# Filler matmuls behind V products split into four of 32 columns, logits by cluster moved there, and x2's block turns sent from another queue

## The chip, the cores and the metric

The kernel runs on one core of one Trainium2 chip. The metric is device time in microseconds (us), as the median of the runs. The profile is of one execution of the same program.

## The reference

Input x has 8 x 512 tokens of 1024 features, all float32. Four steps are each added to the running x, and each works on a layer norm of it:

```python
x = x + attn_a(layernorm(x))   # softmax attention, 32 heads of 32, qkv and output projection
x = x + ffn(layernorm(x))      # dense 1024x1024, masked
x = x + attn_b(layernorm(x))   # causal sigmoid attention, 4 heads of 256, q = k = v = the normed x, bound by sign vectors
x = x + ffn(layernorm(x))      # the same dense layer
```

The mask of the ffn comes from 64 clusters: softmax(10 x centroids^T) per token, hits are the entries above 0.01; a token with no hit gets zeros, and an output feature whose cluster no token hits is zero as well. So the logits by cluster of every token are needed before the first row of ffn's output can be gated.

## The kernel before, in words

Tokens are cut into 32 tiles of 128 (partitions), four tiles to a batch. Five stages follow each other: softmax attention (to about 2600 us of the profile), its tail, the first dense layer (to about 3113 us), sigmoid attention (to about 3465 us), the second dense layer.

**Softmax attention** runs over 64 units: a unit is one batch and one group of four heads (`GH` = 4, `HD_A` = 32). The order on TensorE is written out by hand in the loop over `n`. For each of the four key tiles i of unit n it has: `rows_step` (scores of unit n + 1 with queries as rows, L830, whose maximum VectorE takes, L831), filler, `keys_step` (scores of unit n with keys as rows, L858 and L861, whose exp ScalarE takes, L863), and filler again. At i = 0 `values_step` (V products `av`, L885) and `normalize` (the sums of the softmax `den`, L897, and VectorE's division, L900 on) of unit n - 1 stand between `keys_step` and the filler; at i = 2 `values_step` of unit n. Scores use the array as four row groups of 32 rows (32*128 in the profile); V products and `den` use it as four column groups of 32 columns (128*32), one for each head, each head writing its own 32 partitions of one PSUM tile.

**The filler** is a queue of pieces, each with a weight in us; `between` takes as many as the place's share (`FILLER_SHARES`) allows. In it lie the projections of unit n + 2 (`project_pieces`; q and k L638, V L659, in the first batch L574 and L593), the output projection of the batch before (`out_pair`, L768), and for each finished tile of the attention its norm, its turn (`turn_pieces`, L277) and its cluster logits (`Clusters.pieces`): `by_cluster` puts `logitsT` in two column groups of 64 (128*64, L307), ScalarE copies it (`lT`), and `by_token` (L313) adds the halves and turns them. These products are 128*128. Their PSUM tiles come from the ring `ps_m` of three, which `den` shares.

**The dense layers** run over 16 pairs of tiles: seven products of Strassen-Winograd form (k = 0 to 6), each of four chunks of 512 columns (L1181). ScalarE copies the first into `u` (L148), VectorE adds the others (L142). PSUM has five buffers here. While pair p is multiplied, the tiles of pair p - 1 are normed on ScalarE (`scale`, L240), transposed in 32x32 blocks on VectorE (`turn_blocks`, L1411) and sent to DRAM as `xT2`, four DMAs for each tile, from ScalarE's queue (L1415). SyncE (SP) carries the loads: `load_turned` (L1112) and `load_x` (L1118) of pair p + 2, and at the last pair `load_head` (L1220) and `load_x2` (L1438) for the sigmoid attention. VectorE forms the sums of a pair's left side (L1128) and gates the finished pair (L1194 to L1196).

**Sigmoid attention** runs over 32 heads: scores `csc` (L1240), sigmoid on ScalarE into `at` (L1245), GpSimd's causal select (L1248), values `o` (L1259). `keys` scales the next head's `k` on ScalarE (L1232); `value` makes `cn` on ScalarE and GpSimd (L1226). The last two block turns of x2 are made in steps s = 2 and 3.

Of the kernel before, what the change touches and what calls it, by code (L numbers as in the profile page):

```python
# [22 lines left out]
P = 128  # L23
# [261 lines left out]
        return [(0.45, half(0)), (0.45, half(1))]  # L285


class Clusters:


# [3 lines left out]
        self.hits = fixed.tile([P, NCL], F32, name=f"hits_{name}")  # L294
        self.logits = {}

    def pieces(self, t, xT, later=None):

        nc, (b, i), st, ps_m = self.stage.nc, divmod(t, TPB), {}, self.stage.ps_m

        def by_cluster():
            acc = ps_m.tile([P, P], F32, tag="mm", name="logitsT")
            for c in range(NC):
                half = ts(c % 2, NCL)
                nc.tensor.matmul(acc[half, :], self.cT[:, c, :], xT()[:, c, :], start=(c < 2), stop=(c >= NC - 2))  # L307
            st["lT"] = self.pool.tile([P, P], F32, tag="lT", name=f"lT_{self.name}_{t}")
            nc.scalar.copy(st["lT"], acc)

        def by_token():
            acc = ps_m.tile([P, NCL], F32, tag="mm", name="logits")
            nc.tensor.matmul(acc, st["lT"], self.stage.cst.twice, start=True, stop=True)  # L313
            if i == 0:
                self.logits[b] = self.pool.tile([P, TPB, NCL], F32, tag="lg", name=f"lg_{self.name}_{b}")
            nc.scalar.activation(self.logits[b][:, i, :], acc, AF.Copy, scale=INV_TEMP)
            if i == TPB - 1:
                steps = self.softmax(b)
                if later is None:
                    for step in steps:  # L320
                        step()
                else:
                    later(steps)

        return [(1.3, by_cluster), (0.25, by_token)]
# [61 lines left out]
def softmax_attention(tc, cst, stage, filler, clusters, pools, dr, late, args):  # L387
# [54 lines left out]

    once = [partial(ow_source, RIGHT[k], c) for k in UPPER for c in range(half)]
    ows = Stream(nc, owpool, OW_BUFS, [P, S], "ow", once * (2 * B - 1))
    used, side, tiles, held = {"w": 0}, deque(), deque(), []

    def first_norm():

# [27 lines left out]
    def norm_tasks(b):  # L476
# [48 lines left out]
            scaled[4:],  # L525
        ]

    first_w = {}

    def load_first(g, kinds):  # L530
# [34 lines left out]
    def first_pieces(n):  # L565


        g, st, pieces = n, state.setdefault(n, {}), []

        def qk(t, c):  # L570
            def go():
                if c == 0:
                    st["acc"] = ps_m.tile([P, S], F32, tag="mm", name="mm")
                nc.tensor.matmul(  # L574
                    st["acc"], first_w[t, g, c // half][:, c % half, :], xTs[0][:, c, :],
                    start=(c == 0), stop=(c == NC - 1),
                )
                if c == NC - 1:
                    o = st["qk"[t]] = qkpool.tile([P, S], F32, tag=f"qk{t}", name=f"qk{t}_{n}")
                    bias = qkvb_s[:, t * NC + g : t * NC + g + 1]  # L580
                    if t == 0:
                        nc.vector.tensor_scalar(o, st["acc"], bias, None, ALU.add)
                    else:
                        nc.scalar.activation(o, st["acc"], AF.Identity, bias=bias)

            return go

        def v(i, k):
            def go():
                if i == 0 and k == 0:  # L590
                    st["acc"] = ps_m.tile([P, TPB, P], F32, tag="mm", name="mm")
                for c in range(half):
                    nc.tensor.matmul(  # L593
                        st["acc"][:, i, :], xTs[0][:, k * half + c, ts(i, P)], first_w[2, g, k][:, c, :],
                        start=(k == 0 and c == 0), stop=(k == 1 and c == half - 1),
                    )
                if i == TPB - 1 and k == 1:
                    st["v"] = vpool.tile([P, TPB, P], F32, tag="v", name=f"v_{n}")
                    nc.scalar.copy(st["v"], st["acc"])

            return go

        def sums():
            qk = [first_w.pop((t, g, k)) for k in range(2) for t in range(2)]
            steps = sum_weights("qk", g, *qk) + [partial(load_first, g + 2, (0, 1))]
            if g % 2:
                steps += sum_weights("v", g // 2, *(first_w.pop((2, g - 1 + m, k)) for k in range(2) for m in range(2)))
            steps.append(partial(load_first, g + 2, (2,)))
            side.extendleft(reversed(steps))

        for t in range(2):
            pieces += [(0.86, qk(t, c)) for c in range(NC)]
        return pieces + [(0.87, v(i, k)) for i in range(TPB) for k in range(2)] + [(0.0, sums)]
# [9 lines left out]
    def project_pieces(n):  # L623
# [9 lines left out]
        def qk(k, c0):  # L633
            def go():
                if c0 == 0:
                    st["acc"] = ps_m.tile([P, 2 * P], F32, tag="mm", name="mm")
                for c in (c0, c0 + 1):
                    nc.tensor.matmul(  # L638
                        st["acc"], weights.tiles[base + EARLY.index(k)][:, c, :], left(k)[:, c, :],
                        start=(c == 0), stop=(c == half - 1),  # L640
                    )
                if c0:
                    if k == 0:
                        for t in range(2):
                            st["qk"[t]] = qkpool.tile([P, S], F32, tag=f"qk{t}", name=f"qk{t}_{n}")
                    q, kk = st["q"], st["k"]
                    bias = [qkvb_s[:, t * NC + g : t * NC + g + 1] for t in range(2)]
                    gather(nc, k, st["acc"], q[:, lo], kk[:, lo], q[:, hi], kk[:, hi], bias, early=True)
                    weights.done(base + EARLY.index(k))

            return go

        def v(k, at, i):
            def go():
# [1 line left out]
                    st["acc"] = ps_m.tile([P, 2, P], F32, tag="mm", name="mm")  # L656
                w = weights.tiles[at]
                for c in range(half):
                    nc.tensor.matmul(  # L659
                        st["acc"][:, i, :], left(k)[:, c, ts(i, P)], w[:, c, :], start=(c == 0), stop=(c == half - 1)  # L660
                    )
                if i == 1:
# [38 lines left out]
    def out_pair(q, pools, base, last):  # L701
# [61 lines left out]
        def mm(idx, c):  # L763
            def go():
                k, at = UPPER[idx], base + idx * half + c
                if c == 0:
                    st["acc"] = ps_m.tile([P, S], F32, tag="mm", name="mm")
                nc.tensor.matmul(  # L768
                    st["acc"], st["left"][LEFT[k]][:, c, :], ows.tiles[at], start=(c == 0), stop=(c == half - 1)
                )  # L770
                if last:
                    ows.done(at)
                if c == half - 1:
                    done(k)

            return go
# [23 lines left out]
    def tile_pieces(t, r):  # L800
# [13 lines left out]
        def keep():  # L814
# [1 line left out]

        return (
            stage.norm_pieces(lambda: r, xn, scalar=True) + stage.turn_pieces(xn, xT, keep, vector=False),
            clusters.pieces(t, xT, None if t >= NTILE - TPB else held.extend),
        )  # L820

    def rows_step(n, qt):
# [84 lines left out]

    places = [0]

    def between(sides=True):  # L910

        if sides:
            for _ in range(-(-len(side) // places[0])):
                side.popleft()()
            places[0] -= 1
        filler.take()

    def mix_tile(near=False):
        norm, logits = tiles.popleft()
        filler.mix(norm[:2], 0 if near else 2, 2 if near else 5)  # L920
        filler.mix(norm[2:], 9 if near else 14, 3)
        filler.mix(logits, 16 if near else 22, 4)

    def weave(pieces, products):

# [28 lines left out]
    for n in range(units):  # L954
# [13 lines left out]
            filler.add(weave(project_pieces(ahead), products), mark=ahead)  # L968
        else:
            filler.add(weave([], products))  # L970
        if tiles:
            mix_tile(n == units - 1)
        for c in OUT_SUMS.get(n, ()):
            side.extend(ow_sum_tasks(c))
        if b + 1 < B:
# [10 lines left out]
        for i in range(TPB):  # L986
# [12 lines left out]
                sum_step(n, i)  # L999
            if i == 0 and n > 0:  # L1000
                values_step(n - 1, 1)
                normalize(n - 1)
            if i == 2:
                values_step(n, 0)
            between(False)
        if n + 1 < units:
            split_max(n + 1)
        if ahead < units:
# [264 lines left out]
def block_body(tc, long, dr, args, out):  # L1273
# [117 lines left out]
    def x2_pair(p):  # L1391
# [10 lines left out]
        for t in tiles:  # L1402
            xn, xT, _ = turned_tile(t, dr.xT2)
            scale = (0.0, lambda xn=xn, t=t: stage.rescale(xn(), dense1.x[t], keep(t)))
            turns.append((scale, (0.0, partial(turn_blocks, t, xn, xT))))
        return turns

    def turn_blocks(t, xn, xT):

        blocks = xT().rearrange("p c t -> p (c t)")  # L1410
        nc.vector.transpose(blocks, xn())  # L1411
        dst = dr.xT2[t].rearrange("(j q) (c i t) -> i q c j t", j=P // 32, c=NC, i=P // 32)
        for i in range(P // 32):
            src = blocks[ts(i, 32)].rearrange("q (c j t) -> q c j t", c=NC, j=P // 32)
            nc.scalar.dma_start(dst[i], src)  # L1415

    def x3_pieces(t):

# [28 lines left out]
    for p in range(pairs):  # L1447
        pieces = dense1.products(p) if p > 1 else left_over if p == 1 else []
        for k, (scale, turn) in enumerate(turns):
            pieces.insert(max(len(pieces) - 8, 14) + 5 * k, turn)  # L1450
        at = max(len(pieces) - 19, 12)
        pieces[at:at] = [scale for scale, _ in turns]
        if p == 1:
# [30 lines left out]
    for s in range(heads + 1):  # L1484
# [23 lines left out]
            by_token = turned[1][1:]  # L1508
        run_held()
        if s in (2, 3):  # L1510
            run([turns[s - 2][1]])
        t = s + TPB - 1
        if TPB <= t < NTILE:
            sig.value(t, x2, keep(t))
# [88 lines left out]
```

## Time and profile before

| | us |
|---|---|
| median of 3 runs | 3873.09 (3871.13 to 3873.58) |
| profiled execution | 3871.99 |
| its span | 3870.2 |
| TensorE busy (matmuls) | 3810.0 |
| VectorE busy | 2507.8 |
| ScalarE busy | 942.1 |
| GpSimd busy | 620.1 |
| granted TensorE clock | 0.996 |

A span is from the first to the last instruction; 1.8 us of the profiled execution lie around it. PE is TensorE's matmuls, PEld its weight loads, DVE VectorE, ACT ScalarE, POOL GpSimd, SP SyncE. An x16 behind a row of matmuls counts what the hardware ran: a float32 product is two passes, each with a weight load. Ends of matmuls are modelled, so that rows overlap; starts are exact.

### The profile page before, as it was taken

What the parts mean: (1) busy time and instruction counts of PE and PEld (TensorE: products, weight loads), DVE (VectorE), ACT (ScalarE), POOL (GpSimd) and SP (SyncE); (2) the same over time, 40 slices, a digit from 0 to 9 for tenths busy, and PEclk for the clock granted to TensorE, in tenths of its full rate; (3) what the DMA queues carried; (4) which work ended last, traced back from release to release, by engine and by line L of the source; (5) the groups of instructions that cost most, each with busy time, mean ns of one, the idle gap of its engine ahead of it and who ended that gap; (6) DMA issues with size and microseconds to landing.
All of it is one profiled execution on the core that took longest, in us unless ns stands there. A gap on an engine that the chain in (4) does not pass through costs nothing.

```text
span 3870.2 us, 51693 instructions
## 1 busy us (share of the span) xinstructions
PE 3810.0 (98%) x20526; PEld 2151.8 (56%) x20526; DVE 2507.8 (65%) x3471; ACT 942.1 (24%) x1044; POOL 620.1 (16%) x609
## 2 busy tenths in 40 slices
PE   8999999999999999999999999998999999999999
PEld 4445555655655555655655556543444467774444
DVE  4667676666666666766766666665788744455666
ACT  1222222222222232222322223222111144430000
POOL 1222111111111111111111111111000045530000
PEclk9999999999999999999999999999999999999999
DMA  5435444544544444454354443347566655554332
GB/s 166 125 110 169 125 140 139 169 135 132 177 132 133 146 147 155 127 173 147 121 166 145 131 136 117 110 148 239 154 172 175 183 157 191 191 188 138 130 131 98
DMA packets 574624, 577.57 MB, mean 149 GB/s; under 512 B 168232, under 2 KB 420144, under 8 KB 574384
## 3 DMA queue, kind: packets, MB, share of 16 engines
q1 hardware_dynamic: 408704, 440.81, 36.7%
q0 software_dynamic: 28240, 100.94, 6.6%
q10 hardware_dynamic: 137440, 32.52, 3.8%
q8 instruction: 164, 2.69, 0.3%
q14 instruction: 76, 0.62, 0.0%
HBM read 439.90 MB, written 134.25 MB: 148 GB/s over the span
## 4 chain that ended last, share of the span: by engine, by line
PE 95%; DVE 2%; DMA 2%; ACT 1%; issue 0%; SPq 0%; ACTq 0%; POOL 0%; DVEq 0%; POOLq 0%
PE dense L1181 19%; PE mm L638 19%; PE mm L768 10%; PE mm L659 9%; PE sc L858 7%; PE sc L830 7%; PE av L885 6%; PE csc L1240 4%; PE o L1259 4%; PE mm L574 3%; PE logitsT L307 2%; PE tp L277 2%; PE sc L861 1%; PE den L897 1%; PE mm L593 1%
## 5 line engine op out<-in xcount | busy, mean ns | idle before, releaser
L831 DVE TENSOR_REDUCE nmax<-sc 128x4 f32<-128x2048 f32 x256 | 586.0, 2289 | 306.0 <-PE sc L830 305.0
L863 ACT ACTIVATE pT<-sc 128x2048 f32<-128x2048 f32 x256 | 480.8, 1878 | 1051.6 <-PE sc L861 1051.6
L638 PE MATMUL mm<-xT,w 128*128 128x256 f32 x1792 | 440.0, 389 | 1.4 <-DVE rden L900 1.4
L872 POOL TENSOR_TENSOR sum<-pT,pT 128x1024 f32<-128x1024 f32 x128 | 304.7, 2407 | 763.3 <-ACT pT L863 763.3
L638 PEld LDWEIGHTS mm<-xT,w 128*128 128x128 f32 x1792 | 327.1, 191 | 128.3 <-DVE rest L838 35.6
L638 PE MATMUL mm<-s,w 128*128 128x256 f32 x1344 | 332.1, 390 | 0.0
L638 PEld LDWEIGHTS mm<-s,w 128*128 128x128 f32 x1344 | 244.1, 190 | 134.3 <-issue 95.7
L858 PE MATMUL sc<-qk,qk 32*128 32x512 f32 x2048 | 292.7, 641 | 8.9 <-DVE nmax L831 8.4
L874 DVE TENSOR_TENSOR sum<-sum,pT 128x2048 f32<-128x2048 f32 x128 | 292.0, 2281 | 0.8 <-ACT pT L863 0.8
L830 PE MATMUL sc<-qk,qk 32*128 32x512 f32 x2048 | 291.9, 640 | 0.1
L142 DVE TENSOR_TENSOR u<-dense,u 128x512 f32<-128x512 f32 x223 | 149.6, 688 | 189.6 <-PE dense L1181 166.4
L768 PE MATMUL mm<-ow,ctxT 128*128 128x512 f32 x512 | 252.1, 612 | 0.5 <-DMA ow<-o_T 0.5
L885 PE MATMUL av<-pT,v 128*32 128x512 f32 x2048 | 246.2, 598 | 0.0
L1181 PE MATMUL dense<-sum,s 128*128 128x512 f32 x512 | 233.8, 597 | 6.5 <-ACT u L148 3.9
L659 PEld LDWEIGHTS mm<-w,xT 128*128 128x128 f32 x1792 | 209.1, 192 | 52.9 <-issue 33.8
L144 DVE SCALAR_TENSOR_TENSOR qk<-mm,qkvb_s,qk 128x256 f32<-128x256 f32 x224 | 107.5, 480 | 188.5 <-PE mm L638 186.2
L659 PE MATMUL mm<-w,xT 128*128 128x128 f32 x1792 | 220.5, 278 | 0.0
L768 PE MATMUL mm<-ow,c 128*128 128x512 f32 x360 | 172.6, 610 | 2.8 <-DMA ow<-o_T 2.8
L1181 PE MATMUL dense<-wT_s,dT_b 128*128 128x512 f32 x384 | 171.4, 593 | 1.6 <-DMA dT_b<-xT 1.6
L1181 PE MATMUL dense<-wT_s,dT_a 128*128 128x512 f32 x384 | 171.0, 593 | 0.0
L1181 PEld LDWEIGHTS dense<-sum,s 128*128 128x128 f32 x512 | 97.0, 191 | 128.5 <-issue 112.7
L659 PEld LDWEIGHTS mm<-w,s 128*128 128x128 f32 x1344 | 155.8, 192 | 20.1 <-issue 19.4
(229 smaller groups left out, 4688.9 us busy)
## 6 DMA issues: line engine op xcount, KB each, us to landing
w<-in_qkvw SPq DMA_DIRECT2D x252, 256.0 KB, 2.9
ow<-o_T SPq DMA_DIRECT2D x240, 256.0 KB, 3.5
w<-qk_T SPq DMA_DIRECT2D x224, 256.0 KB, 2.6
ow<-in_ow SPq DMA_DIRECT2D x180, 256.0 KB, 3.0
w<-v_T SPq DMA_DIRECT2D x112, 256.0 KB, 2.7
x<-in_x SPq DMA_DIRECT2D x32, 512.0 KB, 5.0
xT<-nT POOLq DMA_DIRECT2D x32, 512.0 KB, 4.2
dT_a<-xT SPq DMA_DIRECT2D x32, 512.0 KB, 5.5
```

The lines of the kernel that those rows point to most:

```text
L638: nc.tensor.matmul(st["acc"], weights.tiles[base + EARLY.index(k)][:, c, :], left(k)[:, c, :], start=(c == 0), stop=(c == half - 1),)
L659: nc.tensor.matmul(st["acc"][:, i, :], left(k)[:, c, ts(i, P)], w[:, c, :], start=(c == 0), stop=(c == half - 1))
L768: nc.tensor.matmul(st["acc"], st["left"][LEFT[k]][:, c, :], ows.tiles[at], start=(c == 0), stop=(c == half - 1))
L830: nc.tensor.matmul(sc[:, h, :], st["q"][rows, ts(qt, P)], st["k"][rows, :], start=True, stop=True)
L831: nc.vector.tensor_reduce(st["nmax"][:, qt, :], sc, AX.X, ALU.max, negate=True)
L858: nc.tensor.matmul(sc[:, h, :], st["k"][rows, ts(kt, P)], st["q"][rows, :], start=True, stop=False)
L863: nc.scalar.activation(pT, sc, AF.Exp, scale=SCALE_A)
L872: nc.gpsimd.tensor_tensor(st["sum"][:, h, :], st["pT", 0][:, h, :], st["pT", 1][:, h, :], ALU.add)
L874: nc.vector.tensor_tensor(st["sum"], st["sum"], st["pT", kt], ALU.add)
L885: nc.tensor.matmul(st["av"][rows, :], st["v"][:, kt, rows], pT[:, h, :], start=(kt == 0), stop=(kt == TPB - 1))
L1181: nc.tensor.matmul(st["acc"], st["left"][LEFT[k]][:, c, :], self.w[RIGHT[k]][:, c, :], start=(c == 0), stop=(c == half - 1),)
L1240: nc.tensor.matmul(sc[:, AT_OFF[i] : AT_OFF[i] + n], k[:, c, ts(i, P)], xT[:, c, i * P :], start=(c == 0), stop=(c == 1),)
```

## The change

Three things are edited.

1. `product` stands in for the matmul of the projections (q, k, V and output). Where `narrow` is set, it issues four matmuls, one for each group of 32 columns of the left side, into the four 32-partition parts of the same PSUM tile. `between` sets it for the third filler place of i = 0 (behind `values_step` and `normalize`) and that of i = 2 (behind `values_step`), from unit 1 on.
2. In the attention's units `by_cluster` is no longer mixed into the filler of its unit. It waits (`waiting`, `ready`) for i = 0 of the next unit and runs there between `values_step` and `normalize`; `by_token` is put six pieces on in the filler. For the attention's tiles `logitsT` is made in four column groups of 32 (`width=HD_A`).
3. The block turns of x2 become two pieces, `turn` (VectorE's transpose) and `send` (the four DMAs, now from SyncE). In a pair's 28 products the turns stand two to three products earlier, the sends three pieces behind them.

```diff
+    def block_pieces(self, x, box, dram):
+        n = P // 32
+        def turn():
+            self.nc.vector.transpose(box().rearrange("p c t -> p (c t)"), x())
+        def send():
+            blocks = box().rearrange("p c t -> p (c t)")
+            dst = dram.rearrange("(j q) (c i t) -> i q c j t", j=n, c=NC, i=n)
+            for i in range(n):
+                self.nc.sync.dma_start(dst[i], blocks[ts(i, 32)].rearrange("q (c j t) -> q c j t", c=NC, j=n))
+        return [(0.0, turn), (0.0, send)]
...
-    def pieces(self, t, xT, later=None):
+    def pieces(self, t, xT, later=None, width=NCL):
...
             for c in range(NC):
-                half = ts(c % 2, NCL)
-                nc.tensor.matmul(acc[half, :], self.cT[:, c, :], xT()[:, c, :], start=(c < 2), stop=(c >= NC - 2))
+                for j in range(NCL // width):
+                    rows = ts(c % 2 * (NCL // width) + j, width)
+                    nc.tensor.matmul(
+                        acc[rows, :], self.cT[:, c, ts(j, width)], xT()[:, c, :], start=(c < 2), stop=(c >= NC - 2)
+                    )
...
+    narrow = [False]
+
+    def product(out, lhsT, rhs, **flags):
+        if narrow[0]:
+            for j in range(GH):
+                nc.tensor.matmul(out[ts(j, HD_A)], lhsT[:, ts(j, HD_A)], rhs, **flags)
+        else:
+            nc.tensor.matmul(out, lhsT, rhs, **flags)
...
-                nc.tensor.matmul(
+                product(
                     st["acc"], first_w[t, g, c // half][:, c % half, :], xTs[0][:, c, :],
...
-    def between(sides=True):
+    def between(sides=True, form=False):
...
+        narrow[0] = form
         filler.take()
+        narrow[0] = False
...
-        filler.mix(logits, 16 if near else 22, 4)
+        if wait:
+            waiting.append(logits)
+        else:
+            filler.mix(logits, 16 if near else 22, 4)
...
+        ready.extend(waiting)
+        waiting.clear()
         if tiles:
-            mix_tile(n == units - 1)
+            mix_tile(n == units - 1, ahead < units)
...
                 values_step(n - 1, 1)
+                if ready:
+                    by_cluster, by_token = ready.popleft()
+                    run([by_cluster])
+                    filler.mix([by_token], 6, 1)
                 normalize(n - 1)
             if i == 2:
                 values_step(n, 0)
-            between(False)
+            between(False, form=i in (0, 2) and n > 0)
...
         for k, (scale, turn) in enumerate(turns):
-            pieces.insert(max(len(pieces) - 8, 14) + 5 * k, turn)
+            for j, piece in enumerate(turn):
+                pieces.insert(max(len(pieces) - 10, 14) + 4 * k + 3 * j, piece)
...
         if s in (2, 3):
-            run([turns[s - 2][1]])
+            run(turns[s - 2][1])
```

The other four calls of the matmul in `first_pieces`, `project_pieces` and `out_pair` become `product` in the same way.

More of the change, by code (lines that the diff above doesn't have):

```diff
@@ L444, in softmax_attention @@
     ows = Stream(nc, owpool, OW_BUFS, [P, S], "ow", once * (2 * B - 1))
-    used, side, tiles, held = {"w": 0}, deque(), deque(), []
+    used, side, tiles, waiting, ready, held = {"w": 0}, deque(), deque(), deque(), deque(), []
     def first_norm():
@@ L592, in go @@
                 for c in range(half):
-                    nc.tensor.matmul(
+                    product(
                         st["acc"][:, i, :], xTs[0][:, k * half + c, ts(i, P)], first_w[2, g, k][:, c, :],
@@ L637, in go @@
                 for c in (c0, c0 + 1):
-                    nc.tensor.matmul(
+                    product(
                         st["acc"], weights.tiles[base + EARLY.index(k)][:, c, :], left(k)[:, c, :],
@@ L658, in go @@
                 for c in range(half):
-                    nc.tensor.matmul(
+                    product(
                         st["acc"][:, i, :], left(k)[:, c, ts(i, P)], w[:, c, :], start=(c == 0), stop=(c == half - 1)
@@ L767, in go @@
                     st["acc"] = ps_m.tile([P, S], F32, tag="mm", name="mm")
-                nc.tensor.matmul(
+                product(
                     st["acc"], st["left"][LEFT[k]][:, c, :], ows.tiles[at], start=(c == 0), stop=(c == half - 1)
@@ L818, in tile_pieces @@
             stage.norm_pieces(lambda: r, xn, scalar=True) + stage.turn_pieces(xn, xT, keep, vector=False),
-            clusters.pieces(t, xT, None if t >= NTILE - TPB else held.extend),
+            clusters.pieces(t, xT, None if t >= NTILE - TPB else held.extend, width=HD_A),
         )
@@ L915, in between, with mix_tile @@
             places[0] -= 1
+        narrow[0] = form
         filler.take()
-    def mix_tile(near=False):
+        narrow[0] = False
+    def mix_tile(near, wait):
         norm, logits = tiles.popleft()
@@ L1404, in x2_pair @@
             scale = (0.0, lambda xn=xn, t=t: stage.rescale(xn(), dense1.x[t], keep(t)))
-            turns.append((scale, (0.0, partial(turn_blocks, t, xn, xT))))
+            turns.append((scale, stage.block_pieces(xn, xT, dr.xT2[t])))
         return turns
[L1408 to L1415, printed above, removed]
     def x3_pieces(t):
```

## Prediction

> **What bounds the kernel now.** I read the page's first part and its chain first, to see which engine carries the end.
>
> ```profile
> PE 3810.0 (98%) x20526; PEld 2151.8 (56%) x20526; DVE 2507.8 (65%) x3471; ACT 942.1 (24%) x1044; POOL 620.1 (16%) x609
> ...
> PE 95%; DVE 2%; DMA 2%; ACT 1%; issue 0%; SPq 0%; ACTq 0%; POOL 0%; DVEq 0%; POOLq 0%
> ```
>
> Then the busy times by stage, asked for the softmax attention without its first and last units:
>
> ```profile
> 420.00:2580.00 2160.00, 2159.36 (x13787) 1275.28 (x13789) 1423.54 (x1891) 576.56 (x584) 309.63 (x186) 1.00 0.45 140
> ```
>
> The columns are PE, PEld, DVE, ACT, POOL, granted clock, DMA share and GB/s. TensorE is without a break (2159.36 of 2160 us) at full clock, VectorE stands at 66%. So only TensorE's own work counts there, and the question is how much of it is not streaming. The timeline of TensorE in one unit answers that:
>
> ```profile
> 1311.24 1.95 PE L638 MATMUL mm<-xT,w 128*128 128x256 f32 x8
> 1313.11 1.14 PE L858 MATMUL sc<-qk,qk 32*128 32x512 f32 x8
> ...
> 1314.40 1.92 PE L885 MATMUL av<-pT,v 128*32 128x512 f32 x16
> 1316.14 1.04 PE L897 MATMUL den<-sum,ones 128*32 128x512 f32 x8
> 1317.11 1.99 PE L638 MATMUL mm<-s,w 128*128 128x256 f32 x8
> 1319.04 1.14 PE L830 MATMUL sc<-qk,qk 32*128 32x512 f32 x8
> ```
>
> Columns: start, duration, then rows*columns of the array in use and the moving shape. The trace shows every fp32 product as two passes. Starts of single matmuls give one pass at 0.429 us for 512 moving columns, 0.216 for 256, and 0.112 (128*128) or 0.109 (logitsT) for 128. In the 128*32 form four matmuls start about 7 ns apart and share one pass: 16 matmuls of av are four passes of 0.429. Between av (1314.40) and den (1316.14) lie 1.74 us = 4 x 0.429 + 0.02: same form, no gap. From L638 at 1317.11 to L830 at 1319.04 lie 1.93 us for 8 x 0.216 = 1.73, so 0.20 too much. Single starts split it: a change of form costs 0.095 us between the streams (0.091 to 0.098 in nearly all pairs of lines), and the first pass after it is longer by 0.104 us in a 128*128 or score product (320 ns in place of 216), by 0.051 in logitsT, by 0.024 in av. Inside one form (L848 to L638) the gap is 2 to 3 ns.
>
> The logits by cluster have a third form, 128*64, with two turns of their own:
>
> ```profile
> 1211.72 1.09 PE L307 MATMUL logitsT<-nT,cT_s 128*64 128x128 f32 x16
> 1212.74 1.13 PE L638 MATMUL mm<-s,w 128*128 128x256 f32 x4
> 1213.80 1.14 PE L830 MATMUL sc<-qk,qk 32*128 32x512 f32 x8
> ```
>
> Of 1.02 us until L638, 8 x 0.109 = 0.87 stream; L638's four passes need 0.86 and take 1.06.
>
> For the second part I read TensorE's and ScalarE's timelines where the first dense stage meets the sigmoid attention, the largest stalls of the trace:
>
> ```profile
> 3072.73 3.60 PE L1181 MATMUL dense<-sum,dT_a 128*128 128x512 f32 x8
> 3080.18 5.40 PE L1181 MATMUL dense<-sum,s 128*128 128x512 f32 x8 [3.85 <-ACT u L148]
> 3085.41 3.60 PE L1181 MATMUL dense<-wT_s,s 128*128 128x512 f32 x8
> ...
> 3112.88 4.48 PE L1240 MATMUL csc<-cxT,k 128*128 128x512 f32 x16
> 3125.38 6.38 PE L1240 MATMUL csc<-cxT,k 128*128 128x512 f32 x16 [8.03 <-ACT k L1232]
> 3131.59 4.48 PE L1259 MATMUL o<-cn,at 128*128 128x256 f32 x20
> 3135.91 4.26 PE L1240 MATMUL csc<-cxT,k 128*128 128x512 f32 x15
> ```
>
> ```profile
> 3061.16 18.33 ACTq L1415 DMA_DIRECT2D xT<-T  x8
> 3079.54 0.59 ACT L148 COPY u<-dense 128x512 f32<-128x512 f32 x1 [27.36 <-DMA xT<-T]
> ...
> 3108.08 14.07 ACTq L1415 DMA_DIRECT2D xT<-T  x8
> ...
> 3123.48 1.24 ACT L1245 ACTIVATE at<-csc 128x1280 f32<-128x1280 f32 x1
> ```
>
> Both times ScalarE is issuing the eight sends of x2's block turns, and what TensorE waits for stands behind them in ScalarE's queue: the PSUM copy u (L148), then the sigmoid at and the key scaling k. In the 13 pairs between, the same copy comes late too (13 us idle each), but five PSUM buffers hide it: a pair takes 24.03 us = 56 x 0.429, all streaming.
>
> **Part 1: narrow products behind V products.** The orders of instructions of both kernels on TensorE, counted with the prices above: before has 1255 changes of form (551 into 128*128, 512 into scores, 128 into 128*32, 64 into logitsT), after 1108 (428, 512, 136, 32). So 123 fewer entries at 0.095 + 0.104 = 24.5 us, 32 fewer into 128*64 at 0.146 = 4.7, and 8 more into 128*32 at 0.119 = 1.0. Saved: **28.2 us**. As a test of the prices: all streams of before come to 3594 us and its 1255 changes to 236; with the trace's 64 us of longer stalls that is 3894, 0.6% over the span.
>
> Added are matmuls, not passes: 125 products of 512 columns, 330 of 256 and 92 of 128 become four matmuls each, and 32 logitsT become 32 matmuls in place of 16. A narrow pass of 512 is measured (av, 0.429, as in 128*128): nothing. Narrow passes of 256 and 128 are not in the trace. Lower bound: -3 ns at 128 (0.109 against 0.112). Upper bound: matmuls issue no faster than logitsT does, 54.6 ns each (16 in 0.87 us), so four take 218 ns: +2 ns at 256, +108 at 128, where 184 passes of products and 256 of logitsT run: 47.5 us. I take 0, because issue was never what held logitsT (two streams of 0.109 did) and because the sequencer's waits ahead of den (L897) and of the next L638 stand 139 ns apart in the trace, with eight weight loads and eight matmuls of den between: 17 ns a pair where 27 are needed.
>
> [...]
>
> LogitsT now stands between av and den. Den and VectorE's chain behind it (rden, L900) come 0.87 us later; who waits for that is the next av, half a unit away, and a PSUM buffer of the ring of three. By the order after, no buffer is reused within 1.7 us that wasn't before. ScalarE's copy lT then queues behind exp (1.88 us), which started before av (1.72) and is over. The fillers that cover VectorE's maximum (2.29 us) stay as long (shortest 2.35 in both orders), so no score step should become late. I subtract 1.5 us: before 420 us VectorE holds TensorE at times (2.4 us for nmax at 304.9), and of the some 3 us saved there half may only lengthen such waits.
>
> **Part 2: sends by SyncE.** Removed from ScalarE: 128 issues of 0.73 us median (2.3 in the worst stretch). First stall: L1181 would have gone on at 3072.73 + 3.43 = 3076.16 and finished k = 5 at 3079.59; the next product starts at 3085.41. Saved: **5.8 us**, since u is then copied at once. Second: at would follow csc's end (3117.2), k 1.1 later, and csc(0,1) start 1.90 after at, as in the trace: 3119.2 to 3123.5. Then the late one is GpSimd: its select on at stands behind VectorE's gating of the last pair (3124.88 to 3125.91 in this timing), the two v products of 4.66 behind it end at 3130.6, and the last of the o product follows at 3131.1, where the trace has 3135.91. Saved: **4.8 us**; 1 or 2 us of slow clock could be lost in the idle time.
>
> Where they go: SyncE gets, per pair, eight issues (5.8 us; 18.3 at worst) ahead of the four loads for pair p+2, and waits for the VectorE transposes first. The loads were issued at 2884.09; the second transpose ended at 2889.97, so they go out at about 2893 to 2899, land in 5.5 to 7 us, and VectorE wants them at 2915.6: 10 us to spare. Load_head(0) moves behind them too, to about 3062, and its key scaling is due at about 3085 in the shortened timing. The transposes stand one VectorE addition earlier, 1.2 us in an engine with five PSUM buffers of slack. Taken as nothing; ends: 0 and 1 us per pair (13).
>
> **Sum.** The profiled execution took 3871.99 (span 3870.2): 3871.99 - 28.2 + 1.5 - 5.8 - 4.8 = 3834.7. The median of the runs is 1.1 above the profiled one: **3836 us**, 1.0% faster.
>
> **The rivals.** (a) Short narrow passes are bound by issue, the upper bound above: 3836 + 47.5 = 3883, slower by 0.3%. It decides against the change from 85 ns more per 128-column pass (37 us over 440). For it: nothing in the trace streams four at once in 0.11 us. Against: the 139 ns. 11%. [...] (b) VectorE becomes the bound in the attention and takes half of the 28: 3850. For it: it waits little around nmax in single units (22.7 us of weight loads held, 24 times). Against: 66% busy, covers unchanged. 10%. (c) SyncE's sends make dense loads late, 1 us per pair, and the gains of part 2 are gone: 3836 + 10.6 + 13 = 3860. 7%. (d) The narrow products don't save the turn, because an accumulation that changes form pays it elsewhere: 3836 + 26.7 = 3863. Against: av to den. 4%. The forecast itself: 68%.
>
> **How the numbers follow.** Some 0.2% (7.7 us) is what a measurement of this kernel can tell from no change. The forecast's own range is 3827 (second stall and its slow clock gone altogether, 3 ns per short pass) to 3846; up to 3852 it takes in (b): together 78%, and the low end of (a) makes it 8 in 10. Faster: forecast, (b), (c) and half of (d), 0.87; same: the other half of (d) and 0.01 of (a), 0.03; slower: 0.10.
>
> **What the profile would show.** Products of the narrow branch as 128*32 (a piece of two 256-column products: x16 in 0.86 us), the first of them 0.86 us after den's start (0.97 now); passes at 0.216 and 0.11 us. LogitsT 128*32 x32 in 0.87 us between av and den. No stall over 1 us at u L148, and csc(0,1) 2 us behind csc(0,0). I am wrong if a narrow piece of 256 columns lasts over 0.95 us, if idle time of TensorE before scores grows, or if L1181 waits for dT or x.

## The result, and the profile after

| | before | after |
|---|---|---|
| median of the runs beside each other, us | 3872.1 | 3839.8 (3838.2 to 3842.4) |
| ratio | | 0.9919 [0.9902, 0.9936] |
| profiled execution, us | 3871.99 | 3842.35 |

Faster by 0.8%; 3836 was predicted, with 3827 to 3852 as its range. The profiled execution after is the slowest of its four runs, so the median is 3.8 us above the forecast, and the profiled time 7.6 above the sum of 3834.7. Where these 7.6 us lie is what the experiments were to find out.

The busy times of the page, and the first line of its chain:

```profile
PE 3783.0 (98%) x24320; PEld 2103.6 (55%) x24320; DVE 2505.8 (65%) x3471; ACT 943.4 (25%) x1044; POOL 614.9 (16%) x609
...
PE 89%; DVE 7%; DMA 1%; issue 1%; SPq 1%; ACT 0%; POOL 0%; DVEq 0%; ACTq 0%; POOLq 0%
```

There are 3794 more matmuls on TensorE and 27.0 us less busy time. VectorE's share of the chain rose from 2% to 7%: that is new. The busy times of the attention say where:

```profile
420.00:2550.00 2130.00, 2122.52 (x16862) 1225.41 (x16859) 1409.54 (x1869) 573.69 (x581) 302.11 (x185) 1.00 0.48 142
```

TensorE now idles 7.48 us in this stretch, where it idled 0.64 of 2160 before. One piece behind V products and `den`, in the timeline of TensorE:

```profile
1220.98 1.92 PE L915 MATMUL av<-pT,v 128*32 128x512 f32 x16
1222.72 1.06 PE L325 MATMUL logitsT<-nT,cT_s 128*32 128x128 f32 x32
1223.59 1.04 PE L927 MATMUL den<-sum,ones 128*32 128x512 f32 x8
1224.96 1.93 PE L554 MATMUL mm<-s,w 128*32 128x256 f32 x32 [0.32 <-DVE qk L144]
1226.82 1.14 PE L860 MATMUL sc<-qk,qk 32*128 32x512 f32 x8
```

The form no longer turns from av to the filler. Starts of single matmuls give the narrow passes 0.429 us for 512 columns, 0.216 for 256 and 0.109 for 128, logitsT's as well, with no gap behind `den` (two passes of 0.429 from 1142.96, the narrow product at 1143.81); 32 matmuls of 256 columns take 1.86 us until L860. That is what was forecast. New is the wait of 0.32 us on VectorE's `qk` ahead of the next filler product.

The stretch where the dense stage meets the sigmoid attention, on TensorE, then what was issued on SyncE's queue (L300 are the sends of the block turns):

```profile
3087.84 4.48 PE L1282 MATMUL csc<-cxT,k 128*128 128x512 f32 x16
3094.25 6.28 PE L1282 MATMUL csc<-cxT,k 128*128 128x512 f32 x16 [1.94 <-ACT k L1274]
3100.37 2.32 PE L1301 MATMUL o<-cn,at 128*128 128x256 f32 x10
3103.24 1.99 PE L1301 MATMUL o<-cn,at 128*128 128x256 f32 x8 [0.56 <-POOL cn L1268]
3105.57 0.70 PE L1301 MATMUL o<-cn,at 128*128 128x256 f32 x2 [0.33 <-POOL cn L1268]
```

```profile
3057.70 6.74 SPq L300 DMA_DIRECT2D xT<-T  x8
3064.49 1.70 SPq L1262 DMA_DIRECT2D cxT<-xT  x2
```

The stall at `u` (3.85 us of idle before, and a granted clock of 0.5 for 3.41 us from 3081.2) is gone: TensorE streams from 3039.77 to 3087.84 without a break. The 8.03 us before the second `csc` are 1.94, and the 6.83 us at half clock there (from 3122.2) are 3.41 (from 3095.5). GpSimd's `cn` is what comes late next.

With TensorE's starts of the same work in both profiled executions the 29.6 us divide so:

| stretch | saved, us | forecast |
|---|---|---|
| attention and tail, to the start of dense pair 14 | 19.2 | 26.7 |
| from there to the first `csc` | 5.8 | 5.8 |
| from there to the end of its `o` | 4.8 | 4.8 |
| rest | -0.2 | 0 |

The miss lies in the attention. TensorE's waits there, from 430 to 2400 us, with total, count and longest (before has none in that stretch; `nmax` is VectorE's maximum of the scores):

```profile
PE sc L888 <- DVE nmax L861: 4.9, 6, 0.9
PE mm L554 <- DVE qk L144: 1.9, 6, 0.3
```

The kernel of e4 below has the same order on TensorE and almost none of these waits. Against its starts, the waits ahead of scores cost 0.76 to 1.02 us in five batches and 0.50 in the sixth, and those of the filler behind `den` 0.53 us in each of six: 5.3 + 3.2 = 8.5 us.

The waits alone don't give the miss. Up to the last block of scores 28.0 us of changes of form were priced, and the starts show 16.7 gained, 11.3 less: 8.5 are the waits, about 2 are changes of form around the logits that were priced too high (e4 below), and 0.8 are missing before 422 us already. In the tail behind the scores 2.5 us come back where the forecast has 0.2: the granted clock is at half there for 10.2 us in before (records of 3.41 us at 2671.6 and 6.83 at 2705.8) and for 6.8 in after (3.41 each at 2655.2 and 2689.3). That differs from run to run (6.8 us in e1, 10.2 in e2), so about 2 us of the 19.2 are luck.

### The profile page after: what moved, and what is told of

It is laid out like the page before. It is cut to its first block, busy times and chain, and to the rows that moved or that the text cites. A ratio compares the mean times of both kernels' runs of the same rounds, so it can differ in the third digit from the quotient of the medians.

```text
span 3840.6 us, 59277 instructions
## 1 busy us (share of the span) xinstructions
PE 3783.0 (98%) x24320; PEld 2103.6 (55%) x24320; DVE 2505.8 (65%) x3471; ACT 943.4 (25%) x1044; POOL 614.9 (16%) x609
## 4 chain that ended last, share of the span: by engine, by line
PE 89%; DVE 7%; DMA 1%; issue 1%; SPq 1%; ACT 0%; POOL 0%; DVEq 0%; ACTq 0%; POOLq 0%
PE mm L556 33%; PE dense L1223 18%; PE sc L888 7%; PE mm L554 7%; PE sc L860 7%; PE av L915 6%; PE o L1301 4%; PE csc L1282 4%; PE tp L277 1%; PE logitsT L325 1%; PE sc L891 1%; DVE nmax L861 1%; PE den L927 1%; DVE sum L904 1%; DVE xT L534 1%
## 5 line engine op out<-in xcount | busy, mean ns | idle before, releaser
L556 PE MATMUL mm<-xT,w 128*128 128x256 f32 x1716 | 421.9, 389 | 1.6 <-DVE rden L930 1.6
L556 PEld LDWEIGHTS mm<-xT,w 128*128 128x128 f32 x1716 | 311.3, 190 | 132.1 <-issue 42.7
L860 PE MATMUL sc<-qk,qk 32*128 32x512 f32 x2048 | 292.0, 640 | 0.1
L556 PEld LDWEIGHTS mm<-w,xT 128*128 128x128 f32 x1648 | 193.5, 192 | 51.1 <-issue 41.2
L144 DVE SCALAR_TENSOR_TENSOR qk<-mm,qkvb_s,qk 128x256 f32<-128x256 f32 x224 | 107.6, 480 | 151.2 <-PE mm L554 76.2
L556 PE MATMUL mm<-w,xT 128*128 128x128 f32 x1648 | 205.5, 278 | 0.0
L556 PE MATMUL mm<-ow,ctxT 128*128 128x512 f32 x376 | 188.9, 617 | 0.3 <-DMA ow<-o_T 0.2
L556 PE MATMUL mm<-s,w 128*128 128x256 f32 x760 | 182.1, 386 | 0.0
L556 PEld LDWEIGHTS mm<-s,w 128*128 128x128 f32 x760 | 140.6, 190 | 53.1 <-issue 23.5
L556 PE MATMUL mm<-w,s 128*128 128x128 f32 x1344 | 165.1, 277 | 0.0
```

Source lines behind the costliest of these rows:

```text
L556: nc.tensor.matmul(out, lhsT, rhs, **flags)
L860: nc.tensor.matmul(sc[:, h, :], st["q"][rows, ts(qt, P)], st["k"][rows, :], start=True, stop=True)
```

## The experiments

Medians, and ratios to before, whose median beside them was 3870.5 to 3871.7 us:

| run | what it is | us | ratio |
|---|---|---|---|
| e1 | part 2 alone | 3861.4 | 0.9974 [0.9963, 0.9984] |
| e2 | narrow filler alone | 3849.3 | 0.9943 [0.9931, 0.9956] |
| e3 | move of the logits alone | 3875.3 | 1.0013 [1.0004, 1.0022] |
| e4 | after, norm of the next batch on GpSimd | 3831.0 | 0.9896 [0.9881, 0.9911] |
| e5 | after without the move of the logits | 3840.4 | 0.9923 [0.9909, 0.9936] |
| e6 | after, logitsT behind `den` | 3839.9 | 0.9922 [0.9909, 0.9936] |
| e7 | after, all filler narrow | 3881.2 | 1.0029 [1.0019, 1.0040] |
| e8 | e4, filler narrow in nearly all places | 3869.6 | 0.9997 [0.9988, 1.0007] |
| e9 | e4, narrow also where 256 or 512 columns move | 3823.3 | 0.9878 [0.9865, 0.9891] |
| e10 | e4, narrow also where 128 columns move | 3854.6 | 0.9962 [0.9950, 0.9974] |
| e11 | after, cluster softmax queued sooner | 3836.2 | 0.9911 [0.9898, 0.9925] |

**The parts alone (e1, e2, e3).**

e1:

```diff
-            clusters.pieces(t, xT, None if t >= NTILE - TPB else held.extend, width=HD_A),
+            clusters.pieces(t, xT, None if t >= NTILE - TPB else held.extend),
...
-            mix_tile(n == units - 1, ahead < units)
+            mix_tile(n == units - 1, False)
...
-            between(False, form=i in (0, 2) and n > 0)
+            between(False)
```

> The kernel before with part 2 alone: x2's block turns as two pieces, their DMAs from SyncE. TensorE's order is that of the kernel before. By the prediction's terms the stalls at u (5.8 us) and at csc(0,1) (4.8 us) go and nothing comes: 3872 - 10.6 = 3861.5 us. If the sends made the dense loads late (1 us a pair), 3875. Theory A and theory B of the other runs say the same here.

Measured 3861.4, 9.6 us under before. Its waits from 2900 to 3200 us are those of after:

```profile
PE csc L1282 <- ACT k L1274: 1.9, 1, 1.9
PE o L1301 <- POOL cn L1268: 0.9, 2, 0.6
```

e2, with the block turns as in before and the `clusters.pieces` line of e1 too:

```diff
-            mix_tile(n == units - 1, ahead < units)
+            mix_tile(n == units - 1, False)
...
-            turns.append((scale, stage.block_pieces(xn, xT, dr.xT2[t])))
+            turns.append((scale, (0.0, partial(turn_blocks, t, xn, xT))))
```

> The kernel before with narrow filler behind V products alone; logits by cluster as before (two groups of 64, mixed into the filler), sends from ScalarE. Its order has 1165 changes of form in place of 1255, 19.7 us less at the prices of the prediction. The changed kernel has some 8.7 us of new stalls of TensorE on VectorE in the attention. Theory A: they come from the narrow filler, since TensorE runs faster into VectorE's bursts: 3872 - 19.7 + 6 to 9 = 3858 to 3861 us. Theory B: they come from the logits, which stand ahead of den, hold a PSUM buffer there and move 1.3 us of work out of the filler: 3852.5 us, without new stalls.

Measured 3849.3, 21.7 us under before, and TensorE's waits from 430 to 2400 us are none, as in before. So the faster filler alone brings VectorE into no difficulty.

e3, with `turn_blocks` in the same way and the move kept:

```diff
-            between(False, form=i in (0, 2) and n > 0)
+            between(False)
```

> The kernel before with the logits by cluster alone moved behind V products and made in groups of 32; filler 128*128 everywhere, sends from ScalarE. Its order has 1231 changes of form, 3.7 us less. Theory A: 3868 us, no new stalls. Theory B: the stalls come with it, 3.7 us gained and 6 to 9 lost: 3874 to 3877 us, with TensorE waiting for VectorE at the same score steps as in the changed kernel.

Measured 3875.3: a small loss in place of a small gain. Its trace has the new waits (nmax 3.9 us in six, `qk` 1.9 in six). They come with the logits, not with the filler. The three parts alone make -9.6 - 21.7 + 4.3 = -27.0; together they make -32.3. The difference fits the prices: behind logitsT the narrow filler needs no change of form, and the changes saved are 28.2 us together but 19.7 + 3.7 apart, 4.8 less.

**After without the move (e5).**

```diff
-            clusters.pieces(t, xT, None if t >= NTILE - TPB else held.extend, width=HD_A),
+            clusters.pieces(t, xT, None if t >= NTILE - TPB else held.extend),
...
-            mix_tile(n == units - 1, ahead < units)
+            mix_tile(n == units - 1, False)
```

> The kernel after without the move of the logits (parts 1 and 3 stay: narrow filler products and SyncE's sends; logitsT is mixed into the filler as 128*64 again). By its order on TensorE it has 1165 changes of form, 216.4 us by the prices of the prediction, against 1108 and 207.9 in the kernel after: 8.5 us more. Theory A (the new stalls before scores and behind den, 7.5 us in all, belong to the logits move): they go, so 3839.8 + 8.5 - 7.5 = 3841, and no wait of 0.49 us behind den and none of 1.1 us before scores once per batch. Theory B (the stalls come from the filler running faster, whatever lies in it): they stay, 3848.

Measured 3840.4, and no wait of TensorE in 430 to 2400 us: Theory A. Inside the changed kernel the move gains 8.5 us of forms and pays about as much in waits. Its net is nothing that these runs can tell from zero.

**What VectorE is late with (e4, e6, e11).** VectorE's timeline of after, up to a late `nmax`, and TensorE's behind it:

```profile
1169.15 0.28 DVE L370 TENSOR_SCALAR lg_a<-lg_a 128x256 f32<-128x256 f32 x1
1169.80 0.58 DVE L379 TENSOR_REDUCE some<-lg_a 128x64 f32<-128x256 f32 x1
...
1181.61 2.48 DVE L534 TENSOR_TENSOR xT<-xT,rows 128x1024 f32<-128x1024 f32 x2
...
1188.82 2.28 DVE L861 TENSOR_REDUCE nmax<-sc 128x4 f32<-128x2048 f32 x1
```

```profile
1186.49 3.72 PE L556 MATMUL mm<-xT,w 128*128 128x256 f32 x16
1191.16 1.14 PE L888 MATMUL sc<-qk,qk 32*128 32x512 f32 x8 [0.94 <-DVE nmax L861]
```

From 1166.94 to 1192 VectorE has no idle time over 0.10 us. It runs L534 (scale and bias of the norm of batch b + 1's rows) and the last steps of the cluster softmax (L370 to L380, 1.4 us). In e5 those softmax steps run a unit earlier, and the same `nmax` is in time. Its VectorE:

```profile
1126.97 0.28 DVE L370 TENSOR_SCALAR lg_a<-lg_a 128x256 f32<-128x256 f32 x1
...
1186.00 2.28 DVE L861 TENSOR_REDUCE nmax<-sc 128x4 f32<-128x2048 f32 x1
```

and its TensorE, which goes on to the scores without a wait:

```profile
1184.89 3.72 PE L556 MATMUL mm<-xT,w 128*128 128x256 f32 x16
1188.55 1.14 PE L888 MATMUL sc<-qk,qk 32*128 32x512 f32 x8
```

Three edits test this. e4:

```diff
-            nc.vector.tensor_tensor(part, part, rows, (ALU.mult, ALU.add)[k])
+            nc.gpsimd.tensor_tensor(part, part, rows, (ALU.mult, ALU.add)[k])
```

> The changed kernel with the eight steps per batch that apply the next batch's norm (xT times and plus rows, 1.22 us each on VectorE) moved to GpSimd, where a product of 128x1024 took 2.3 us. Both theories put the new stalls on VectorE's queue; if the norm's steps are what fills it in the two units of each batch where they stand, TensorE's waits of 1.1 and 0.5 us there go: 3840 - 8 = 3832 us. If the queue is filled by the gathers and sums that every unit has, 3840. If GpSimd's own sums (sum of pT, 2.4 us each) come late behind the 2.3 us steps, 3845 or more.

Measured 3831.0, 8.8 us under after. Of its waits from 430 to 2400 us this is left:

```profile
PE sc L888 <- DVE nmax L861: 0.4, 1, 0.4
```

So it is VectorE's load that costs, and GpSimd has room for the norm (302.11 of 2130 us busy in the attention of after). The one wait left is the sixth, in the last batch, which no norm of a next batch follows (at 2366 us in after); what causes it isn't shown. Is it the delay of `den` by logitsT? e6:

```diff
+                normalize(n - 1)
                 if ready:
                     by_cluster, by_token = ready.popleft()
                     run([by_cluster])
                     filler.mix([by_token], 6, 1)
-                normalize(n - 1)
```

> The kernel after with logitsT issued behind normalize in place of ahead of it: same 1108 changes, same work; den and VectorE's division behind it come 0.87 us earlier. Theory A (it is den's delay that makes VectorE's chain late, with the norm steps in the same queue): the 1.1 us before scores once per batch shrinks by about 0.9, in five batches and at 863 us some 5 us: 3835; the 0.49 us (now between logitsT and the filler product) stay, since logitsT still takes one of the three mm buffers ahead of that product. Theory B (the norm steps in VectorE's queue alone do it, wherever den stands): both waits stay as they are, 3840.

Measured 3839.9, with both waits to the tenth as in after (4.9 and 1.9): Theory B. The 0.87 us that `den` is later cost nothing, as the prediction took it. Then the softmax, e11:

```diff
-            clusters.pieces(t, xT, None if t >= NTILE - TPB else held.extend, width=HD_A),
+            clusters.pieces(t, xT, None if t >= NTILE - TPB else lambda steps: soon[0].extend(steps), width=HD_A),
...
+    soon = [side]
...
     normalize(units - 1)
+    run(enumerate(side))
+    side.clear()
+    soon[0] = held
     yield
```

> The kernel after with the cluster softmax of a batch (the VectorE steps at L357 to L380, 2.9 us, which the move of the logits puts one unit later than before) queued as soon as the batch's last logits are there, in place of at the start of the next unit. TensorE's order is the same, 1108 changes of form. Theory A (it is these steps, 1.4 us of them in front of the unit in which VectorE also norms the next batch, that make nmax late): the waits of 0.6 to 1.1 us before scores once per batch (6.0 us in six) go, those of 0.49 behind den (2.9 us, a PSUM buffer held until VectorE's gather) stay: 3834. Theory B (the norm steps alone are enough, the softmax only happens to be near): both stay, 3840.

Measured 3836.2, 3.7 us under after, which the intervals of the two ratios don't separate; the waits do. Those before scores shrink from 4.9 us to 0.7, those on `qk` stay:

```profile
PE mm L555 <- DVE qk L144: 1.9, 6, 0.3
PE sc L889 <- DVE nmax L862: 0.7, 2, 0.4
```

Theory A in its places; its 3834 was 2 us too low. So in five of the six batches the late `nmax` needs both, the norm and the softmax in one stretch. The waits on `qk` have another cause: logitsT takes one of the three `mm` buffers next to `den`, so the filler product behind them needs the one that VectorE's gather L144 frees, and at 1223.29 that gather stands behind an L534 of 1.22 us. They stay with logitsT on either side of `den` (e6) and go when L534 leaves VectorE (e4) or logitsT leaves the place (e5).

**How far the narrow form carries (e7, e8, e10, e9).** In after only 92 products of 128 columns are narrow. e7 makes all filler narrow:

```diff
-            between()
+            between(form=True)
             if i == 0:
                 turn_max(n)
-                between()
+                between(form=True)
...
-            between(False, form=i in (0, 2) and n > 0)
+            between(False, form=True)
```

> The kernel after with the filler of every place in the narrow form, not only that behind V products. By its order it has 1367 changes of form (185 into 128*128, 512 into scores, 638 into 128*32, 32 into 128*64), 219.3 us by the prices, 11.4 more than after, though the dear entries into 128*128 are gone; 1760 products of 128 columns run as 128*32, 0.109 us a pass in place of 0.112 if they stay as short as the 46 groups of after: 10.0 us less. Theory A (narrow passes cost what wide ones do even in long runs, only changes count): 3839.8 + 11.4 - 10.0 = 3841. Theory B (long runs of four short matmuls per pass are held by issue or by weight loads): each of the 3520 passes of 128 columns some 10 ns longer gives 35 us, 3876 or more.

Measured 3881.2: Theory B's side, by another way than it says. The passes stay short: of 3374 periods from one pass of 128 columns to the next, 3203 are within 10 ns of 0.109 us. Much of the time is in few gaps, 25 of them together 21.6 us, at which the profile sees nothing released ("issue"). e8 is e4's kernel with the narrow form in all places but the two around `turn_max`:

```diff
-            between()
+            between(form=i > 0)
             if i == 0:
                 turn_max(n)
...
-            between(False, form=i in (0, 2) and n > 0)
+            between(False, form=True)
```

> The kernel of e4 (after, with the norm's scale and bias on GpSimd) with the filler narrow in all places but the two around the query maximum of i = 0: 1240 changes of form, but of the 1240 only 185 into 128*128 at 0.199 us and 511 into 128*32 at 0.119: 204.2 us against 207.9. Theory A (narrow passes cost 0.109 at 128 columns in long runs too): 3831.0 - 3.7 - 10.0 = 3817. Theory B (long runs are held by issue or by loads): over 3831, by the amount that the passes are over 0.109 (35 us for 10 ns).

Measured 3869.6, 52 us over Theory A. TensorE's waits from 130 to 2600 us in e8 begin:

```profile
PE mm L554 <- issue: 25.2, 13, 4.5
```

e9 and e10 divide e8's places by what moves in them. The place ahead of `keys_step` i is p = 2i, the one behind it p = 2i + 1. e9 takes p = 2, 3, 4 in the units where no product of 128 columns lies there; e10 has the same edit with `return p in (6, 7)`:

```diff
+    def narrow_at(n, p):
+        mid = ((2,), (4,), (3, 4), (2, 3, 4))[n % 4]
+        return p in ((2, 3, 4) if n < 12 or n > 58 else mid if n < 56 else (2,))
...
-            between()
+            between(form=narrow_at(n, 2 * i))
...
-            between(False, form=i in (0, 2) and n > 0)
+            between(False, form=(i in (0, 2) and n > 0) or narrow_at(n, 2 * i + 1))
```

> The counterpart of e9: the kernel of e4 with the narrow form in the two places of i = 3, which hold nearly all the products of 128 columns (7024 passes' matmuls in place of 368). 1109 changes of form, 198.0 us against 207.9, and 10.0 us less for passes of 0.109 in place of 0.112. Theory A: the interruptions of e8 (27.9 us in 15 gaps between passes of 128 columns, and the slow clock behind them) come here too, in the first units of each batch: 3831.0 - 9.9 - 10.0 = 3811 and 30 to 45 us on top, 3841 to 3856. Theory B (they need the instructions of all the narrow places together): 3811 to 3825.

> The kernel of e4 with the narrow form in 127 more places of the filler, those between two blocks of scores whose products all move 256 or 512 columns (places behind the scores of i = 1 and ahead of those of i = 1 and i = 2, by the unit's place in its batch); products of 128 columns stay as in e4. By the order on TensorE 1111 changes of form, 302 of them into 128*128 in place of 428, 198.2 us against 207.9. Theory A (the interruptions without a releaser in e7 and e8 come only with long runs of narrow products of 128 columns, which need some 37 matmuls a us): 3831.0 - 9.7 = 3821. Theory B (they come with the number of instructions in all): part of the 9.7 is lost, 3825 to 3835, and TensorE shows waits on issue.

Measured 3854.6 for e10, in Theory A's range and 43 us over the price without gaps, and 3823.3 for e9, 7.7 us under e4 where 9.7 were priced. e9 shows no wait on issue. TensorE of e10 in one interrupted unit:

```profile
1132.71 2.81 PE L554 MATMUL mm<-w,xT 128*32 128x128 f32 x90
1136.15 0.29 PE L554 MATMUL mm<-w,xT 128*32 128x128 f32 x1 [0.63 <-issue]
1136.62 1.18 PE L554 MATMUL mm<-w,xT 128*32 128x128 f32 x34 [0.17 <-issue]
1139.75 0.64 PE L554 MATMUL mm<-w,xT 128*32 128x128 f32 x3 [1.96 <-issue]
```

The next two units run equal products without a gap. What differs is the DMA traffic. From 1127.8 to 1140.3 us, and then one unit later, from 1168.5 to 1181, it is:

```profile
DMA packets 1715, 1.24 MB, mean 99 GB/s; under 512 B 1119, under 2 KB 1119, under 8 KB 1714
```

```profile
DMA packets 1012, 2.11 MB, mean 169 GB/s; under 512 B 114, under 2 KB 115, under 8 KB 1011
```

Ten times as many packets under 512 B in the interrupted one. They are those of one DMA, which SyncE issues once per batch, seven times in all, and which moves 4 KB in packets of 4 bytes:

```profile
1127.37 0.38 SPq L526 DMA_DIRECT2D rows<-ln_rows  x1
```

In e7, e8 and e10, all gaps over 0.3 us between narrow passes of 128 columns (23, 15 and 17 of them) begin 6 to 12 us behind one of these seven issues, and each of the seven has at least one such gap behind it in all three kernels. In after, e4 and e9 the same DMA goes out in the same place, wide products of 128 columns run there, and there is no such gap. Another candidate is the page's queue of kind "instruction", if its packets come late: it moved 193 packets in after, 231 in e9 (which has no gap), 273 in e10, 325 in e8 and 346 in e7. Beside three of e10's seven groups of gaps one such packet took 2.6 to 4.2 us, beside the other four none took over 1.1. No run moved or left out that DMA or was made to change those packets: where the gaps fall is shown, what causes them stays open.

e9 is the fastest kernel of this study, 3823.3 us, 1.2% under before.

## Why the prediction was right, and where it missed

- **Changes of form.** Right, and the main term. The narrow filler alone was priced at 19.7 us and gave 21.7 (e2); in its starts from 422 to 2318 us of before it gained 13.55 us where 13.5 are priced. Narrow passes of 256 and 512 columns cost what wide ones cost, 0.216 and 0.429 us, as taken. The changes around the logits were priced too high: e4, in which the new waits of that stretch are gone, gained 19.7 of 21.5 us there. e9 used the same prices for 127 more places and gave 7.7 of 9.7 us; those 2 us aren't explained.
- **Part 2.** Right to 0.1 us in both stalls, GpSimd's `cn` as the next to be late included; e1 gave 9.6 us against 10.6. SyncE's sends cost nothing that shows: the pairs of the first dense layer stay at 24.03 us and none waits for a load. Rival (c) is out.
- **"So no score step should become late."** This step failed, and the prediction's own sign of being wrong came: idle time of TensorE before scores grew from nothing to 4.9 us between 430 and 2400 us. The prediction checked that the fillers covering VectorE's maximum stay as long, not what stands ahead of the maximum in VectorE's queue. It followed logitsT, `den` and the copy `lT`, and left out the last consumer of the logits: the cluster softmax, which moves one unit later with them and meets the norm of the next batch (e11, e4). Its price was nothing; measured are 5.3 us.
- **"No buffer is reused within 1.7 us that wasn't before."** Counted in TensorE's order it says nothing of when VectorE frees the buffer: 0.53 us six times, 3.2 us.
- **The 1.5 us** taken as absorbed before 420 us can't be told from these runs. Up to 422 us of before the starts show 2.6 us gained of 3.4 priced in after, but 1.9 in e4 and 4.6 in e5. The stretches of 3.41 us at half clock there differ from one execution to another: they begin at 16.1, 306.2 and 415.4 us in before, at 16.7, 125.9 and 306.8 in after.
- **The total** came within 3.8 us in part by luck. Waits of 8.5 us that the prediction put at nothing, and the logits' changes of form, stand against 2.5 us that the tail gave back and the 1.5 us set aside.
- **Rival (a)** is out for this kernel, with four matmuls in 0.109 us: 27 ns each on average, weight loads beside them. But e7, e8 and e10 show a near relative of (a), gaps in long runs of short narrow products, and with such runs in the places of i = 3 the kernel lost 24 us (e10 against e4). **Rival (b)**, VectorE in the way in the attention, is what happened in small: 8.5 us of the 28 in place of half. **Rival (d)** is out: no gap from `den` to the narrow product (0.86 us from start to start, two passes of 0.429).

## What to carry to other kernels

Where matmuls of different tilings alternate, count the changes of form and price them from starts of single matmuls (0.12 to 0.20 us each by those of before). In this kernel, splitting a product to stay in the neighbour's form cost nothing that shows for moving sizes of 256 and 512 columns (0.216 and 0.429 us a pass, wide in before and narrow in after; e2, e9), and was dear in long runs at 128 (e10, 3854.6 us against 3831.0 in e4). When a step is moved, follow its results to the last consumer, and look on that consumer's engine at what it meets in the new place. An engine that is 66% busy over a stage can be full for 25 us on end, as VectorE is here, and that is where a moved step of 1.4 us turns into a wait.

## What was not expected of the hardware

Four narrow matmuls of 128 columns stream in 0.109 us with their weight loads, some 37 matmuls a us. Yet in long rows of them (up to 128 in one view) TensorE is at times interrupted for up to 4.5 us (e8) with no semaphore waited for (e7, e8, e10). All such gaps over 0.3 us between narrow passes of 128 columns begin 6 to 12 us behind the same small DMA of 4 KB.

The granted clock falls behind some of these groups of gaps, two of the seven in e7 and four in e10. In e7 it is 0.73 from 1148 to 1152 us and 0.50 from 1152 to 1156, behind four gaps of 0.4 to 1.8 us. In e10 it is 0.72 from 1140 to 1150 us, and the eight matmuls of 256 columns that start at 1142.34 take 3.38 us to the next start, where the same eight in after, at 1136.00, take 1.83. So such a group can cost more than the length of its gaps.
